# Sandwich layer on one core: 68 pages instead of 71, three more in a branch, and another order for the batches' ends

## The chip, the cores and the metric

The kernel runs on one core of a Trainium2 chip. The metric is the device time of one execution in microseconds (us), lower is better. A profile is one execution taken by the hardware profiler; times inside it are counted from its first instruction.

## The reference, cut to what matters

The input `x` has 16 batches of 512 tokens with 256 numbers each. The layer is

```
x = x + layernorm(block_sparse_attention(layernorm(x)))
x = x + layernorm(ffn(layernorm(x)))
```

and the change lies in the second line. For each token, with `xn` the input of `ffn` after its own layer norm:

```
abel   = gelu(xn @ abel_w + abel_b)
logits = xn @ moe_gate_w + moe_gate_b           # 8 experts
topw, topi = top_k(logits, 2); topw = softmax(topw)
moe    = sum over the two of topw * (gelu(xn @ ew1[e] + eb1[e]) @ ew2[e] + eb2[e])
moe    = moe @ expm(gens[0]) @ expm(gens[1]) @ expm(gens[2])
gate   = sigmoid(concat(abel, moe) @ gc_w + gc_b)
out    = residual + abel * (1 - gate) + moe * gate
```

So there are 16 x 512 x 2 = 16384 rows for the experts. How many go to which expert depends on the data.

## The kernel before, in words

**Two stages.** `attention` walks over the batches: projections, scores, weighting, and in `close(b)` the first residual, the dense `abel` part (stored in `lin_d`), the sum (stored in `x1_d`) and `route`, which gives every row a place. The rotations are folded into the experts' second weights (`second_weights`, tiles `w2` and `eb2r`) at the end of this stage.

**Pages.** A page is 256 rows of one expert. `route(b, ...)` counts the rows of each expert over all batches so far (`count`, `filled`: pages opened per expert), opens pages as they are needed, and `close` scatters the rows to their slots in `slots_d` (line 731, an indirect DMA of POOL; eight per batch). An empty slot holds a row number out of bounds, and its row is not stored later. Eight experts with ragged ends need at most 2 x 16 x 512 / 256 + 8 - 1 = 71 pages, the constant `PAGES`.

**The expert stage.** `experts` runs over all pages, full or empty, in a Python loop that is written out in full. For a page, `fetch` reads the expert's number from `whose` into registers of SP, PE and DVE (line 1038), loads `w1` (line 1046) and the 256 rows (line 1050); `flip` transposes the rows on TensorE (line 1061) and scales them on ScalarE (line 1065); `hidden` makes one half of the hidden layer (TensorE line 1078, Gelu on ScalarE line 1086); `result` makes one half of the output (TensorE `eo` line 1096, two VectorE operations lines 1103 and 1109) and scatters it to the tokens' places in `made_d` (line 1112, POOL). Within the loop the hidden layer of page n+1 is written beside the result of page n, half by half.

**The ends of the batches.** `last[b]` is the page by which every row of batch b is sure to be made: 4(b + 1) + 6. `leave(b, ...)` is a Python generator with the closing work of batch b; each `next` writes one step into the loop. Its steps: load `x1` and `abel` (lines 1126, 1128); Gelu of `abel` and its part of the gate (lines 1134, 1138); gather the batch's rows as `moe` from `made_d` (line 1144); sum them (lines 1159, 1160); Tanh for the gate (line 1164) and mixing (lines 1167 to 1181) with the statistics of the last layer norm (lines 373, 374); a power on POOL (line 1195); the shift (lines 1198, 1201) and the norm on ScalarE (line 1203); the last sum and five stores (line 1214, `place` line 156). Every batch that is leaving takes one step per page, in the page's first half:

```python
for batch in leaving:
    next(batch, None)
if n + 2 >= PAGES:
    next(leaving[-2])
```

The last batch works in two parts of two columns each. With 71 pages, batch 14's last page is 66 and batch 15's is 70.

**What sets the order.** `tc.manual_schedule` keeps PE, DVE, ScalarE and POOL in the order in which the program is written: an instruction that waits holds up all behind it on its engine. SP, which issues nearly all plain DMAs, is not in that set: a planner orders its queue, and the queue runs in that order. `scattered` and `gathered` tell the planner which accesses to `slots_d` and `made_d` depend on each other. At the very end the kernel has an `If` on `left` (lines 1300, 1301), which holds a second version of the layer and is not entered with these inputs.

Of the kernel before, what the change touches and what calls it, by code (L numbers as in the profile page):

```python
# [58 lines left out]
EARLY_TURNS = 31  # L59
KNOWN = 32  # L60
# [7 lines left out]
def kernel(ctx: ExitStack, tc: tile.TileContext, a: dict, out: bass.AP):  # L68
# [14 lines left out]
    left = keep.tile([P, 1], I32, name="left")  # L83

# [9 lines left out]
        keep.tile([1, n], I32, name=f"whose{i}") for i, n in enumerate((KNOWN, PAGES - KNOWN))  # L94
# [48 lines left out]
    def asked(slots, i):  # L143

        lo, hi = ((0, KNOWN), (KNOWN, PAGES))[i]
        first = slots_d.bitcast(I32).rearrange("(n g) c -> n g c", g=G)[lo:hi, 0, D + 2]
        gathered(slots, nc.sync.dma_start(whose[i], first.unsqueeze(0)))

    def place(b, t, store=False, part=slice(0, 4)):

        for c, p0, blk, n in RUNS:
            if not part.start <= c < part.stop:
                continue
            here = t[p0 : p0 + n * BLK, c, :]
            there = (out if store else x)[b, blk * BLK : (blk + n) * BLK, :]
            nc.sync.dma_start(*((there, here) if store else (here, there)))
# [245 lines left out]
    def attention(lowered, slots, ffn):  # L402
# [366 lines left out]
        def route(b, lg, rows):  # L769
# [134 lines left out]
            nc.vector.tensor_copy(filled, now)  # L904
            return slot_i
# [122 lines left out]
    def experts(slots, results, judged, ffn, ready):  # L1028
# [8 lines left out]
        def fetch(n):  # L1037
            e = nc.values_load(
                whose[0][0:1, n : n + 1] if n < KNOWN else whose[1][0:1, n - KNOWN : n - KNOWN + 1],
                engines=[ENG.SP, ENG.PE, ENG.DVE],  # L1040
                min_val=0,
                max_val=E - 1,
                skip_runtime_bounds_check_because="each is below E, or 0",
            )
            w1 = four.tile([P, 2 * HID + HID // P], F32, name="w1")
            nc.sync.dma_start(w1, a["w1"][bass.ds(e, 1)].rearrange("e p c -> p (e c)"))
            rows = two.tile([P, 2, ROW], F32, name="rows", bufs=7)
            gathered(
                slots,
                nc.sync.dma_start(  # L1050
                    rows, slots_d[n * G : (n + 1) * G, :].rearrange("(j p) c -> p j c", p=P)
                ),
            )
            return e, w1, rows
# [67 lines left out]
        def leave(b, until, parts):  # L1122
# [7 lines left out]
            gate = small.tile([P, 4], F32, name="gate")  # L1130
            for half in range(2):
                cs = range(2 * half, 2 * half + 2)
                own = abel[:, 2 * half : 2 * half + 2, :]
                nc.scalar.activation(own, own, AF.Gelu)
                yield
                for c in cs:
                    junk = two.tile([P, D], F32, name="junk")
                    nc.vector.tensor_tensor_reduce(
                        junk, abel[:, c, :], gcw[0], 1.0, 0.0, ALU.mult, ALU.add, gate[:, c : c + 1]
                    )  # L1140
            moe = two.tile([P, 2, 4, W], F32, name="moe")
# [11 lines left out]
            g = small.tile([P, 2, 4], F32, name="g")  # L1153
            xi = two.tile([P, 4, D], F32, name="xi")
# [3 lines left out]
            for part in parts:  # L1158
                nc.vector.tensor_tensor(y[:, part], y[:, part], moe[:, 1, part], ALU.add)
                nc.vector.tensor_tensor(gate[:, part], gate[:, part], y[:, part, D], ALU.add)  # L1160
            yield
            for part in parts:

                nc.scalar.activation(g[:, 0, part], gate[:, part], AF.Tanh, bias=gcb, scale=0.5)
            for part in parts:
                for i, sign in ((1, -0.5), (0, 0.5)):
                    nc.vector.tensor_scalar(  # L1167
                        g[:, i, part], g[:, 0, part], sign, 0.5, ALU.mult, ALU.add
                    )


                n = part.stop - part.start
                nc.vector.tensor_tensor(
                    g[:, :, part],
                    g[:, :, part],
                    power[:, b, 1, part].unsqueeze(1).to_broadcast([P, 2, n]),
                    ALU.mult,
                )
                for c in range(part.start, part.stop):
                    for i, (t, to) in enumerate(((y, x1), (abel, xi))):  # L1180
                        nc.vector.scalar_tensor_tensor(  # L1181
                            xi[:, c, :],
                            t[:, c, 0:D],
                            g[:, i, c : c + 1],
                            to[:, c, :],
                            ALU.mult,
                            ALU.add,
                        )
                    moments(small, mv, xi[:, c, :], c)
                    if c in (0, 2):  # L1190
                        yield
# [4 lines left out]
            yield  # L1196
            for part in parts:
# [4 lines left out]
                for c in range(part.start, part.stop):  # L1202
                    nc.scalar.activation(  # L1203
                        xi[:, c, :],
                        xi[:, c, :],
                        AF.Identity,
                        bias=off[:, c : c + 1],
                        scale=rs[:, c : c + 1],
                    )
                    if c == 1:  # L1210
                        yield
            yield
            for part in parts:
                nc.vector.tensor_tensor(x1[:, part], x1[:, part], xi[:, part], ALU.add)
                place(b, x1, store=True, part=part)
            yield
# [25 lines left out]
        last = [(b + 1) * 2 * S // G + E - 2 for b in range(B)]  # L1242
        early = 2
        whole, by_two = [slice(0, 4)], [slice(0, 2), slice(2, 4)]
        until = {}
        least = one.tile([P, 4], F32, name="least")
        with tc.manual_schedule(engines={ENG.PE, ENG.DVE, ENG.Activation, ENG.Pool}):
# [7 lines left out]
            leaving = []  # L1255
            for n in range(PAGES):
                if n + 3 < PAGES:
                    fetched.append(fetch(n + 3))
                if n == KNOWN // 2:
                    asked(slots, 1)  # L1260
                if n + early in last:
                    b = last.index(n + early)
                    leaving.append(leave(b, until, whole if b + 1 < B else by_two))
                if n + 2 < PAGES:
                    xns.append(flip(fetched[n + 2][2]))
# [3 lines left out]
                for half in range(2):  # L1269
                    if n + 1 < PAGES:  # L1270
                        hidden(fetched[n + 1][1], xns[n + 1], later, half)
                    result(e, rows, h, made, half)
                    if half == 0:
                        for batch in leaving:
                            next(batch, None)
                        if n + 2 >= PAGES:
                            next(leaving[-2])
# [5 lines left out]
                elif judged and n == 4:  # L1283
                    judge(least)

            next(leaving[-1])
            for batch in leaving:
                for _ in batch:
# [102 lines left out]
```

## Time and profile before

| | us |
|---|---|
| median of 3 runs | 1401.78 (1399.41 to 1402.66) |
| the profiled execution | 1397.93 |
| its span, first to last instruction | 1396.2 |
| first `flip` of the expert stage starts | 833.41 |
| last `eo` matmuls start, take | 1353.97, 5.38 |
| mean granted TensorE clock | 0.975 of full speed |

PE is TensorE's matmuls, PEld its weight loads, DVE VectorE, ACT ScalarE, POOL GpSimd, SP the engine that issues DMAs. In a table of windows each row is one stretch of time, with the busy time of PE, PEld, DVE, ACT and POOL, then the granted clock, the busy share of the DMA engines and GB/s. A timeline row gives start, duration, engine, line, operation, the tiles it writes and reads, how many instructions were merged, and in brackets how long the engine was idle before it and who released it. A row of a line's instructions gives durations in ns (least, median, most) and first and last start. A row of a DMA queue gives packets, MB and share.

### The profile page before, as it was taken

How to read it: one execution, taken by the hardware profiler on the slowest of the kernel's cores; microseconds unless marked ns; L12 is line 12 of the kernel's file. 1: busy time of each engine (PE TensorE's matmuls, PEld its weight loads, DVE VectorE, ACT ScalarE, POOL GpSimd, SP SyncE). 2: the span in 40 equal slices, each digit the busy share in tenths (PEclk: the TensorE clock that was granted, in tenths of full speed). 3: DMA queues.
4: the chain of work that ended last, by engine and by line, in shares of the span. 5: the costliest groups of instructions: out<-in, count | busy, mean ns of one | idle time of the engine just before them, and what ended most of it. 6: DMA issues, size and time to landing. Idle time of an engine off the chain costs nothing. (4 is left out here: it accounts for less than half of the span.)

```text
span 1396.2 us, 26363 instructions
## 1 busy us (share of the span) xinstructions
PE 1318.2 (94%) x9364; PEld 924.9 (66%) x9364; DVE 837.6 (60%) x2702; ACT 710.8 (51%) x1105; POOL 424.1 (30%) x433
## 2 busy tenths in 40 slices
PE   5999999999999999999998979999999999999990
PEld 2455555556555655555554668888888888888880
DVE  4366867797667668667666623224556555565565
ACT  1556556655665555666665334344444444444441
POOL 1001133323332332333424342223333333333331
PEclk9999999999999999999999989999999999999995
DMA  9971011211121121112101556455767776677732
GB/s 264 283 180 46 32 62 58 73 40 62 55 69 46 47 69 39 69 55 70 54 36 65 215 165 216 138 170 170 246 220 237 242 244 219 225 224 248 227 113 78
DMA packets 119295, 187.46 MB, mean 134 GB/s; under 512 B 12776, under 2 KB 93300, under 8 KB 119028
## 3 DMA queue, kind: packets, MB, share of 16 engines
q1 hardware_dynamic: 104516, 149.87, 34.7%
q0 software_dynamic: 12960, 33.84, 6.7%
q10 hardware_dynamic: 1680, 1.97, 0.5%
q8 instruction: 78, 1.28, 0.4%
q14 instruction: 61, 0.50, 0.1%
HBM read 107.81 MB, written 79.66 MB: 134 GB/s over the span
## 5 line engine op out<-in xcount | busy, mean ns | idle before, releaser
L616 ACT ACTIVATE prob<-score 128x1024 f32<-128x1024 f32 x384 | 372.3, 1021 | 234.0 <-PE score L606 234.0
L1096 PE MATMUL eo<-w,hid 128*128 x1136 | 269.8, 379 | 0.0
L1078 PE MATMUL hid_ps<-xn,w 128*128 128x256 f32 x1136 | 269.7, 381 | 0.0
L1112 POOL DMA_INDIRECT made_d<-made,rows x142 | 163.7, 1152 | 334.6 <-DVE made L1109 221.2
L1096 PEld LDWEIGHTS eo<-w,hid 128*128 128x128 f32 x1136 | 215.6, 190 | 31.1
L606 PE MATMUL score<-qk 32*128 32x512 f32 (+4 forms) x2560 | 231.9, 455 | 1.3 <-DVE qk L536 0.8
L1078 PEld LDWEIGHTS hid_ps<-xn,w 128*128 128x128 f32 x1136 | 211.0, 191 | 26.9 <-ACT xn L1065 0.3
L1103 DVE TENSOR_TENSOR made<-eo,eb2r_b 128x257 f32<-128x257 f32 x142 | 60.5, 426 | 251.1 <-PE eo L1096 224.4
L1086 ACT ACTIVATE hid<-hid_ps,w 128x256 f32<-128x256 f32 x284 | 118.9, 469 | 169.9 <-PE hid_ps L1078 121.2
L627 PE MATMUL att<-prob,vals 128*32 128x512 f32 (+4 forms) x2560 | 180.0, 427 | 0.0
L606 PEld LDWEIGHTS score<-qk 32*128 32x128 f32 x2560 | 119.6, 186 | 78.9 <-issue 36.1
L627 PEld LDWEIGHTS att<-prob,vals 128*32 128x32 f32 x2560 | 76.8, 110 | 135.5 <-issue 113.6
L731 POOL DMA_INDIRECT slots_d<-rows,slot_i x128 | 127.6, 997 | 71.8 <-issue 34.9
L379 POOL TENSOR_TENSOR rs<-rs,halves 128x4 f32<-128x4 f32 x32 | 32.9, 1028 | 327.6 <-DVE rs L378 321.7
L1065 ACT ACTIVATE xn<-flip,beta,gamma 128x256 f32<-128x256 f32 x142 | 72.4, 560 | 92.8 <-PE flip L1061 83.1
L544 PE MATMUL projv<-wv,ht 128*128 128x256 f32 x256 | 64.4, 393 | 4.4 <-DVE vals L551 4.1
L637 ACT COPY outs<-att 128x512 f32<-128x512 f32 x64 | 37.5, 586 | 55.7 <-PE att L627 55.7
L536 DVE SCALAR_TENSOR_TENSOR qk<-proj,owns,added_q 128x512 f32<-128x512 f32 x64 | 45.1, 746 | 34.0 <-PE proj L526 34.0
L526 PE MATMUL proj<-ht,wq 128*128 128x512 f32 x128 | 64.9, 631 | 0.0
L716 PE MATMUL abel<-wa,xn 128*128 128x264 f32 x256 | 63.6, 393 | 0.0
L688 POOL TENSOR_TENSOR power<-spread,halves 128x8 f32<-128x8 f32 x16 | 26.6, 1662 | 119.0 <-DVE spread L684 119.0
L526 PE MATMUL proj<-hk,wk 128*128 128x512 f32 x128 | 62.5, 611 | 0.1
(247 smaller groups left out, 1522.7 us busy)
## 6 DMA issues: line engine op xcount, KB each, us to landing
w<-in_w SPq DMA_DIRECT2D x71, 514.0 KB, 5.6
slots_d<-empty SPq DMA_DIRECT2D x1, 18389.0 KB, 71.2
rows<-slots_d SPq DMA_DIRECT2D x71, 259.0 KB, 3.1
moe<-made_d SPq DMA_DIRECT2D x30, 514.0 KB, 5.0
x_d<-x SPq DMA_DIRECT2D x16, 512.0 KB, 2.6
lin_d<-lin SPq DMA_DIRECT2D x16, 512.0 KB, 3.2
x<-x_d SPq DMA_DIRECT2D x16, 512.0 KB, 7.3
abel<-lin_d SPq DMA_DIRECT2D x16, 512.0 KB, 5.5
```

The source lines that it names most:

```text
L526: nc.tensor.matmul(ps, w[:, k, u * P : (u + 1) * P], src[:, k, :], start=k == 0, stop=k == 1,)
L544: nc.tensor.matmul(ps, ht[:, k, c * P : (c + 1) * P], wv[:, k, :], start=k == 0, stop=k == 1,)
L606: nc.tensor.matmul(ps[t // 2][:, t % 2, at : at + hi - lo], k[32 * t : 32 * t + 32, c * P : (c + 1) * P], q[32 * t : 32 * t + 32, lo:hi], ...
L616: nc.scalar.activation(pr, ps[i], AF.Exp, scale=HD**-0.5)
L627: nc.tensor.matmul(po[32 * t : 32 * t + 32, lo:hi], vals[b % 2][:, c, 4 * g + t, :], got[t // 2][:, t % 2, at : at + hi - lo], start=first ...
L716: nc.tensor.matmul(ps, xn[:, k, c * P : (c + 1) * P], wa[:, k, :], start=k == 0, stop=k == 1,)
L731: scatter = nc.gpsimd.indirect_dma_start(slots_d, bass.IndirectOffsetOnAxis(slot_i[:, r, c : c + 1], 0), rows[:, r, c, :], None, bounds_ch ...
L1065: nc.scalar.activation(xn[:, k, :], ps[:, k].rearrange("p j t -> p (j t)"), AF.Identity, bias=beta[:, k : k + 1], scale=gamma[:, k : k + 1],)
L1078: nc.tensor.matmul(pair[:, m % 2, :], w1[:, k * HID + m * P : k * HID + (m + 1) * P], xn[:, k, :], start=k == 0, stop=k == 1,)
L1086: nc.scalar.activation(h[:, m, :], pair[:, m % 2, :], AF.Gelu, bias=w1[:, 2 * HID + m : 2 * HID + m + 1],)
L1096: nc.tensor.matmul(ps, h[:, m, j * P : (j + 1) * P], w2[:, bass.ds(e, 1), m, :].rearrange("p e d -> p (e d)"), start=m == 0, stop=m == HID ...
L1112: scatter = nc.gpsimd.indirect_dma_start(made_d, bass.IndirectOffsetOnAxis(rows.bitcast(I32)[:, j, D : D + 1], 0), made[:, j, :], None, bo ...
```

## The change

`MOST = 68` pages are run always. The numbers of pages 68 to 70 come from a third `whose` tile, inside a branch that runs these pages on their own, ahead of the loop, if `route` of the last batch has counted more than 68 opened pages (`opened`). The loop and `last` end at page 67, so that batch 14 closes at 66 and batch 15 at 67.

`leave` starts one page earlier and does its steps at a written pace: `paces[0]` says how many steps are taken in the first half of a page, by its distance to the batch's last page, `paces[1]` the same for the second half. `abel * power + x1` is summed into `xi` before the gather; afterwards `(y - abel) * gate` is added to it, where before `y * gate + x1` and `abel * (1 - gate)` were. The last batch's two parts are written interleaved, and its last two stores go on two queues.

```diff
+MOST = 68
@@ tile_sandwich_kernel
+    opened = keep.tile([P, 1], I32, name="opened")
-        keep.tile([1, n], I32, name=f"whose{i}") for i, n in enumerate((KNOWN, PAGES - KNOWN))
+        keep.tile([1, n], I32, name=f"whose{i}")
+        for i, n in enumerate((KNOWN, MOST - KNOWN, PAGES - MOST))
@@ place
+            queue = queues[c % len(queues)]
+            queue.dma_start(*((there, here) if store else (here, there)))
@@ route, at its end
             nc.vector.tensor_copy(filled, now)
+            if b == B - 1:
+                nc.vector.tensor_reduce(used, filled, AX.X, ALU.add)
+                nc.vector.tensor_copy(opened, used)
@@ leave
+            back = power[:, b, 1]
...
+            xi = two.tile([P, 4, D], F32, name="xi")
+            for c in range(4):
+                nc.vector.scalar_tensor_tensor(
+                    xi[:, c, :], abel[:, c, :], back[:, c : c + 1], x1[:, c, :], ALU.mult, ALU.add
+                )
+            yield
+            whole, by_two = [slice(0, 4)], [slice(0, 2), slice(2, 4)]
+            parts = whole if b + 1 < B else by_two
             moe = two.tile([P, 2, 4, W], F32, name="moe")
...
+            def gates(part):
                 nc.vector.tensor_tensor(y[:, part], y[:, part], moe[:, 1, part], ALU.add)
                 nc.vector.tensor_tensor(gate[:, part], gate[:, part], y[:, part, D], ALU.add)
+                nc.scalar.activation(g[:, part], gate[:, part], AF.Tanh, bias=gcb, scale=0.5)
+
+            def other(part):
+                nc.vector.tensor_tensor(
+                    y[:, part, 0:D], y[:, part, 0:D], abel[:, part], ALU.subtract
+                )
+                nc.vector.tensor_scalar(g[:, part], g[:, part], 0.5, 0.5, ALU.mult, ALU.add)
+                nc.vector.tensor_tensor(g[:, part], g[:, part], back[:, part], ALU.mult)
+
+            def mixed(c):
+                nc.vector.scalar_tensor_tensor(
+                    xi[:, c, :], y[:, c, 0:D], g[:, c : c + 1], xi[:, c, :], ALU.mult, ALU.add
+                )
+                moments(small, mv, xi[:, c, :], c)
+
+            def scales(part):
+                (lines 1192 and 1195)
+            def shifts(part):
+                (lines 1198 and 1201)
+            def normed_mix(c):
+                (line 1203)
+            def stored_sum(part, queues=(nc.sync,)):
+                nc.vector.tensor_tensor(x1[:, part], x1[:, part], xi[:, part], ALU.add)
+                place(b, x1, store=True, part=part, queues=queues)
+
+            if b + 1 < B:
+                part = parts[0]
+                gates(part)
+                yield
+                other(part)
+                mixed(0)
+                yield
+                mixed(1)
+                mixed(2)
+                yield
+                mixed(3)
+                scales(part)
+                yield
+                shifts(part)
+                normed_mix(0)
+                normed_mix(1)
+                yield
+                normed_mix(2)
+                normed_mix(3)
+                yield
+                stored_sum(part)
+                yield
+            else:
+                first, second = parts
+                gates(first)
+                other(first)
+                mixed(0)
+                mixed(1)
+                scales(first)
+                gates(second)
+                other(second)
+                shifts(first)
+                normed_mix(0)
+                normed_mix(1)
+                mixed(2)
+                mixed(3)
+                scales(second)
+                stored_sum(first)
+                shifts(second)
+                normed_mix(2)
+                normed_mix(3)
+                stored_sum(second, (nc.sync, nc.scalar))
+                yield
@@ experts, the loop
-        last = [(b + 1) * 2 * S // G + E - 2 for b in range(B)]
-        early = 2
+        last = [min((b + 1) * 2 * S // G + E - 2, MOST - 1) for b in range(B)]
+        paces = [{k: 1 for k in range(-3, 2)}, {}]
+        paces[0].update({2: 3, 3: 2, 4: 2})
+        paces[1].update({4: 1})
+        more = nc.values_load(opened[0:1, 0:1], min_val=0, max_val=PAGES)
+        with tc.If(more > MOST), tc.manual_schedule(engines=in_order):
+            asked(slots, 2)
+            for n in range(MOST, PAGES):
+                e, w1, rows = fetch(n)
+                xn = flip(rows)
+                h = two.tile([P, HID // P, G], F32, name="hid")
+                made = four.tile([P, 2, W], F32, name="made")
+                for half in range(2):
+                    hidden(w1, xn, h, half)
+                for half in range(2):
+                    result(e, rows, h, made, half)
+            def go_on(n, half):
+                for b in leaving:
+                    for _ in range(paces[half].get(n - last[b], 0)):
+                        next(leaving[b])
+
-            for n in range(PAGES):
+            for n in range(MOST):
...
-                if n + early in last:
-                    b = last.index(n + early)
-                    leaving.append(leave(b, until, whole if b + 1 < B else by_two))
+                if n + 3 in last:
+                    b = last.index(n + 3)
+                    leaving[b] = leave(b, until)
...
                     result(e, rows, h, made, half)
-                    if half == 0:
-                        for batch in leaving:
-                            next(batch, None)
-                        if n + 2 >= PAGES:
-                            next(leaving[-2])
+                    if n + 1 < MOST:
+                        go_on(n, half)
...
-            next(leaving[-1])
-            for batch in leaving:
-                for _ in batch:
+            go_on(MOST - 1, 0)
+
+            next(leaving[B - 1])
+            for b in range(B):
+                for _ in leaving[b]:
                     pass
```

## The prediction

> **What bounds the kernel now.** I read the page first, then windows over the expert stage, then the timeline at the stage's start, in the middle of a batch and at its end, and last the line of an existing branch.
>
> ```profile
> PE 1318.2 (94%) x9364; PEld 924.9 (66%) x9364; DVE 837.6 (60%) x2702; ACT 710.8 (51%) x1105; POOL 424.1 (30%) x433
> ```
> ```profile
> 1100.00:1200.00 100.00, 100.00 (x489) 87.64 (x488) 58.06 (x169) 45.64 (x102) 35.87 (x31) 1.00 0.72 228
> 1200.00:1300.00 100.00, 100.00 (x490) 87.64 (x490) 54.58 (x160) 48.20 (x108) 36.98 (x32) 1.00 0.74 237
> ```
> TensorE is the bound of the expert stage: busy 100 of 100 us at the full granted clock, VectorE (third pair) at 55 to 58, ScalarE at 46 to 48. A page's block starts with its `flip`: flips stand at 1193.99 and 1201.36, so one page costs 7.37 us. What is worth time is a page less, or a stall of TensorE.
>
> ```profile
> 807.74 16.37 PEld L1013 LDWEIGHTS w2r<-rot,w2t 128*128 128x128 f32 x76
> 827.22 0.98 POOL L731 DMA_INDIRECT slots_d<-rows,slot_i  x1 [0.30 <-issue]
> 830.38 3.44 SPq L1050 DMA_DIRECT2D rows<-slots_d  x7
> 833.41 1.94 PE L1061 MATMUL flip<-ident,rows 128*128 128x128 f32 x8 [8.89 <-DMA rows<-slots_d]
> ```
> At the stage's start TensorE is idle from 824.1 to 833.4: it waits for the last scatter into `slots_d` to land, then for the first `rows`.
>
> ```profile
> 1353.97 5.38 PE L1096 MATMUL eo<-w,hid 128*128 x24
> 1364.80 0.43 DVE L1103 TENSOR_TENSOR made<-eo,eb2r_b 128x257 f32<-128x257 f32 x1
> 1366.27 2.09 POOL L1112 DMA_INDIRECT made_d<-made,rows  x1 [0.20 <-issue]
> 1369.62 1.91 SPq L1144 DMA_DIRECT2D moe<-made_d  x4
> 1373.18 0.70 DVE L1159 TENSOR_TENSOR moe<-moe 128x514 f32<-128x514 f32 x1 [2.04 <-DMA moe<-made_d]
> 1387.86 0.69 DVE L1214 TENSOR_TENSOR x<-x,xi 128x512 f32<-128x512 f32 x1 [0.29 <-ACT xi L1203]
> ```
> Call the last matmul's end E (1353.97 + 5.38 = 1359.35). The last `made` comes only 5.4 us later, because VectorE, in written order, does batch 14's sums first. Then scatter, gather and batch 15's arithmetic follow in one chain; the last sum ends at 1388.55, E + 29.2, and the span at E + 36.85.
>
> **Does the branch stay untaken?** The reference's routing on its inputs sends 3849, 1182, 1593, 809, 3068, 1176, 2250 and 2457 rows to the eight experts. In pages of 256, rounded up: 16 + 5 + 7 + 4 + 12 + 5 + 9 + 10 = 68, not over 68. The trace says the same. From 1350 to 1397 the queue of indirect transfers moves nothing:
> ```profile
> q0 software_dynamic: 289, 0.00, 0.4%
> ```
> At 48 packets each that is six scatters, those of pages 68 to 70: they carry no row.
>
> **Three pages less.** 3 x 7.37 = 22.1 us of TensorE that nothing else overlaps: E comes 22.1 us earlier.
>
> **The branch.** Each engine gets a register load, a compare and a jump over the three pages. The kernel has such a jump at its end:
> ```profile
> L1301 PEldq COMPARE_BRANCH  x1: 3357/3357/3357, 1357.1 to 1357.1; - x1
> L1301 ACTq COMPARE_BRANCH  x1: 50/50/50, 1387.2 to 1387.2; - x1
> ```
> The row first: 3.36 us on TensorE; on ScalarE 0.05, but its next entry on that line is at 1389.7, 2.5 us later. The Trainium skill ("Runtime: NRT & Kernel Launch", section "Instruction fetch mechanics") gives the reason and speaks against the change: a taken branch beyond the fetched pages waits for an instruction fetch, and control flow at run time is expensive. By that rule alone I would add 3.4 us. By the trace the place matters: TensorE has 9.3 idle us there, so load (0.31) and jump (3.36) after 824.1 end near 828, before 833.4. SP can read the count at about 818.5, when the last routing is done, and is through by about 822.5; its first three loads of `w` (5.6 us to land; issued near 780 before) go out near 823.5 and are there before the first rows. POOL jumps after its last scatter and needs 0.5 + 2.5 + 1.35 (`INC_SWDGE_SEM` of the same line), near 833, and is needed at 846. What is left on the path is VectorE's reduce and copy ahead of the last eight scatters: 2 x 0.2 = 0.4 us. If the cover fails (`rows` waiting for POOL's jump, or `w` late) it is 3 to 4 us. A gain is excluded: the first flip waits for a scatter that comes no earlier. I take +0.4.
>
> **The middle batches.** The arithmetic changes by one 128x1024 subtraction (1.23 us by the row of `moe<-moe`) less two small operations: about +1 us of VectorE per batch, free at 58%. The pace is not free. The gather `moe` still goes out in the page after the batch's last one, but its sum and the Tanh now stand one page earlier. Batch 9, pages 48 and 49:
> ```profile
> 1193.99 0.60 PE L1061 MATMUL flip<-ident,rows 128*128 128x128 f32 x4
> 1195.42 0.98 SPq L1144 DMA_DIRECT2D moe<-made_d  x2
> 1197.54 0.57 SPq L1126 DMA_DIRECT2D x<-x_d  x1
> 1198.09 0.43 DVE L1103 TENSOR_TENSOR made<-eo,eb2r_b 128x257 f32<-128x257 f32 x1 [0.87 <-PE eo L1096]
> 1203.52 1.90 PE L1096 MATMUL eo<-w,hid 128*128 x8
> ```
> The second gather goes out near 1195.9 and lands 5.0 us later, 1200.9. VectorE is free for the sum at 1198.9, so it now waits 2 us. Queued behind it is ScalarE's Tanh, and behind that the next batch's Gelu and the Gelu of page 49's second half, which TensorE's `eo` at 1203.52 needs at its third of four parts (1204.5). Landing 1200.9 + sums 1.5 + Tanh 0.25 + Gelu 0.5 + Gelu 0.45 = 1203.6: 0.9 us to spare. Batches differ. Where the two gathers are issued 1.7 us apart (three of the 14 batches that close among pages, at 1048, 1136 and 1254) it lands 1.3 us later, and TensorE waits 0.3 to 1.2 us, 2.7 together; the others add a few tenths. Over 14 batches I take +3.3 us. With all landings 1 us earlier it is 0.4; with all 1 us later 13. Stores and `made` have room: four `eo` buffers are two pages.
>
> **The end.** Batches 14 and 15 now close one page apart, so almost nothing of batch 14 is covered. Its gather is written after both scatters of the last page, and in the trace a gather waits for every scatter written before it (batch 9's went out at 1195.42, with the landing of page 47's first scatter, though its rows were in by page 46). Relative to E: the last `made` 1.6 (no batch-14 sums ahead, three to four us better), scatter issued 2.35, landed 3.25 later (1366.27 to 1369.5 before) = 5.6; gather issued by 6.1, landed 5.2 later = 11.3. Batch 14: sum and gate 1.45, subtraction 1.25, three small 0.4, four columns of 1.08 (0.48 + 0.43 + 0.18) = 4.3, scale, POOL's power and shift 1.9, four Identity 2.3, sum 1.25: ends at 24.2. VectorE is in written order, so batch 15 (landed long since) starts there: first half 0.9 + 0.7 + 0.4 + 2.15 + 0.2, the second half's gates and shifts 2.3, columns 2.15, power and shift 1.6, Identity 1.3, sum 0.7: about 12.3, ends at 36.4 against 29.2. The last two stores now go on two queues right behind it (0.6 against 1.84 from last sum to last issue): -1.2. Net +5.9. If the gather of 14 starts before the last scatter it is 3; if gathers disturb each other 9.
>
> **Sum.** -22.1 + 0.4 + 3.3 + 5.9 = -12.5 us. The profiled execution took 1397.93 (span 1396.2 and 1.7 around it), which becomes 1385.4. It is 3.85 below the median of the runs, so I put the difference on the median: 1401.78 - 12.5 = 1389.3.
>
> **The rivals.** *Nearly the whole gain*: gathers land a little earlier, no stalls, and the end costs only 2 to 3: -22.1 + 0.4 + 2.5 = -19, 1382.6. For it: batch 15 alone is 3 us shorter by its new order. Against it: batch 14 has lost its cover of four pages.
>
> *Slower, by the gather.* The next batch's loads of `x1` and `abel` (1 MB) are now written in the same step as the gather; before, `x` came out behind it (1197.54). If they go out just ahead, 1 MB at the 230 GB/s of this window is 4.4 us of transfers, of which 2 us would fall on the gather. Each batch then stalls TensorE about 2 us more at the Tanh: 3.3 + 14 x 1.8 = 28, the sum is +12, 1414. It decides from 1.2 us of lateness per batch. Against it: SP waits at the gather for the scatter anyway, and transfers issued before that wait are mostly done by its end.
>
> *The branch is taken.* Expert 4 holds 3068 rows of 3072; five rows routed otherwise would open a 69th page. Three pages without overlap, at 10 to 15 us each, cost 30 to 45: 1425. The empty scatters above speak against it.
>
> *Less*: jump exposed or later landings, -3 to -7, near 1397.
>
> **How the numbers follow.** About 0.2% (2.8 us) is what a measurement of this kernel can tell from none. My forecast (-17 to -7): 0.55. Nearly the whole gain: 0.18. Less, but faster: 0.08. Within 0.2%: 0.04. Slower by the gather: 0.13; branch taken: 0.02. So faster 0.81, same 0.04, slower 0.15. The range leaves out the slower cases and the best twentieth: 1380 to 1399; the likeliest case's own is 1385 to 1395.
>
> **What would show it.** 68 of each page group, 1088 `eo` matmuls; TensorE from the first flip to E 22 us shorter less its stalls; those stalls, if any, at `eo` released by ScalarE in the third page after a batch's last; first flip within 1 us of 833.4; the Tanh's idle time put down to the gate sum and that one's to `moe<-made_d`; batch 14's gather issued near E + 6 and the last sum near E + 36. Wrong would be a first flip past 836, stalls over 10 us together, or a last sum before E + 31.

## The result, and the profile after

The changed kernel took 1407.86 us (median of 12 runs, 1402.62 to 1410.11); the kernel before, on the same chip, 1402.70 (12 runs, 1399.41 to 1405.35). The ratio is 1.0027, 95% interval 1.0014 to 1.0040: slower by 0.27% or some 4 us (the medians lie 5.2 us apart), where 12.5 us less were forecast. The profiled execution took 1402.62, with a span of 1400.8 against 1396.2.

The page's first row, and the two windows in the middle of the stage (columns as in the tables of windows before):

```profile
PE 1297.2 (93%) x9256; PEld 904.4 (65%) x9256; DVE 844.9 (60%) x2692; ACT 700.7 (50%) x1088; POOL 409.8 (29%) x427
```
```profile
1100.00:1200.00 100.00, 100.00 (x491) 87.46 (x490) 60.69 (x168) 46.41 (x106) 32.85 (x30) 1.00 0.74 239
1200.00:1300.00 100.00, 99.72 (x487) 87.07 (x486) 60.45 (x173) 47.00 (x106) 34.91 (x31) 1.00 0.72 227
```

TensorE's busy time fell by 21.0 us: the three pages are gone. The middle is still nearly full; 0.28 us of idle time shows in the second window. So most of the time went at the two ends of the stage. The start of the stage (timeline):

```profile
832.74 0.98 POOL L735 DMA_INDIRECT slots_d<-rows,slot_i  x1 [0.30 <-issue]
835.71 0.34 SPq L1135 DMA_DIRECT2D x<-x_d  x1
...
837.52 0.74 SPq L1135 DMA_DIRECT2D x<-x_d  x1
844.12 0.36 SPq L1055 DMA_DIRECT2D w<-in_w  x1
844.53 0.43 SPq L1059 DMA_DIRECT2D rows<-slots_d  x1
...
848.57 1.09 PE L1070 MATMUL flip<-ident,rows 128*128 128x128 f32 x4 [18.86 <-DMA rows<-slots_d]
```

and, of the instructions of the branch's line, these five rows (duration in ns, first and last start in us; an `EVENT_SEMAPHORE` is a wait of an engine's queue, a `COMPARE_BRANCH` the jump):

```profile
L1300 SPq EVENT_SEMAPHORE  x8: 17/17/17, 838.8 to 843.5; - x8
L1300 PEldq COMPARE_BRANCH  x1: 358/358/358, 827.3 to 827.3; - x1
L1300 ACTq COMPARE_BRANCH  x1: 50/50/50, 830.6 to 830.6; - x1
L1300 POOLq INC_SWDGE_SEM  x1: 618/618/618, 833.0 to 833.0; - x1
L1300 SPq COMPARE_BRANCH  x1: 50/50/50, 838.3 to 838.3; - x1
```

Before, SP sent out the first `rows` 3.16 us behind the start of the last scatter, as soon as it had landed. After, it is 11.79 us (832.74 to 844.53), and these parts add up to it. SP stands 2.97 us in its queue until the scatter has landed, because loads of `x1` and `abel` for batches 0 to 2 are now ahead of the jump, and they too wait for the scatters; 2.60 us go to issuing five of them (835.71 to 838.31); 5.19 us to the waits behind SP's jump (838.31 to 843.5), which end one by one (at 839.4, 840.6, 841.9 and 843.3); 1.03 us to the expert's number and the first `w`. That these waits are for the five loads is read from their number and order; this trace does not show the loads' landings. The trace of e3, with the same branch, does for some: there two of the waits are passed at 835.59 and 836.90, and two of the loads land at 835.58 and 836.89. TensorE, ScalarE and POOL jumped long before, as the prediction had it. SP did not.

The way from the first `flip` to the first `eo` grew as well, by 2.8 us. Of these 2.0 are a second wait of TensorE, ahead of the second page's `flip` (851.66). The rest are slower matmuls: the first 16 of `hid_ps` take 5.80 us, where they took 5.07. They run longer at a low granted clock, the third number from a row's end in these stretches, two of the kernel before (first `flip` at 833.41) and two of the changed one (848.57). The clock is back at full some 4.6 us behind the first `flip` before, and 8.4 after.

```profile
834.00:838.00 4.00, 4.00 (x14) 3.13 (x13) 0.00 (x0) 3.21 (x5) 0.00 (x0) 0.50 1.01 319
838.00:842.00 4.00, 4.00 (x22) 3.54 (x21) 0.00 (x0) 2.45 (x6) 0.00 (x0) 0.99 1.02 410
```
```profile
850.00:854.00 4.00, 2.33 (x8) 2.10 (x9) 0.00 (x0) 3.24 (x6) 0.00 (x0) 0.50 1.00 366
854.00:858.00 4.00, 4.00 (x14) 3.24 (x13) 0.00 (x0) 2.01 (x3) 0.00 (x0) 0.63 1.05 385
```

The end of the stage, some rows from the last matmuls on:

```profile
1352.74 5.54 PE L1105 MATMUL eo<-w,hid 128*128 x24
1358.32 0.43 DVE L1112 TENSOR_TENSOR made<-eo,eb2r_b 128x257 f32<-128x257 f32 x1 [0.22 <-PE eo L1105]
1359.65 1.01 POOL L1121 DMA_INDIRECT made_d<-made,rows  x1 [0.30 <-issue]
1364.71 3.12 SPq L1163 DMA_DIRECT2D moe<-made_d  x6
1369.94 1.23 DVE L1178 TENSOR_TENSOR moe<-moe 128x1028 f32<-128x1028 f32 x1 [8.54 <-DMA moe<-made_d]
1393.53 0.69 DVE L1219 TENSOR_TENSOR x<-x,xi 128x512 f32<-128x512 f32 x1 [1.22 <-ACT xi L1210]
```

Batch 14's sums wait for their gather (8.54 us of idle VectorE), and batch 15's work stands behind them. The last sum ends at E + 35.9, where it was E + 29.2.

A second profile of the changed kernel was taken later (e7, below). The whole by stages, where "scatter" is the start of the last scatter into `slots_d`, E the end of the last matmul and "sum" the end of the last sum (us; differences of the rows of each timeline):

| | before | after | again |
|---|---|---|---|
| start to last scatter | 827.2 | 832.7 | 828.6 |
| scatter to first `flip` | 6.2 | 15.8 | 16.2 |
| first `flip` to first `eo` | 8.9 | 11.8 | 10.9 |
| first `eo` to E | 517.0 | 497.9 | 503.7 |
| E to last sum | 29.2 | 35.9 | 36.4 |
| last sum to end | 7.6 | 6.6 | 6.8 |

The first row's 5.5 us do not belong to the change: the second profile has 1.4, and e1's, with the same first stage, 0.1. In the profiles of the experiments below the last scatter starts between 823.7 (e12) and 834.9 (e9); what sets it was not tried. The second profile is from another chip, where the kernel before took 1394.31 us (median of 15 runs), so its 1404.38 us lie 10 us above that kernel.

### The profile page after: what moved, and what is told of

Same layout as the page of the kernel before. It is cut to its first block, busy times and chain, and to the rows that moved or that the text cites. A ratio compares the mean times of both kernels' runs of the same rounds, so it can differ in the third digit from the quotient of the medians.

```text
span 1400.8 us, 26082 instructions
## 1 busy us (share of the span) xinstructions
PE 1297.2 (93%) x9256; PEld 904.4 (65%) x9256; DVE 844.9 (60%) x2692; ACT 700.7 (50%) x1088; POOL 409.8 (29%) x427
## 3 DMA queue, kind: packets, MB, share of 16 engines
q8 instruction: 78, 1.28, 0.4%
## 5 line engine op out<-in xcount | busy, mean ns | idle before, releaser
L1105 PE MATMUL eo<-w,hid 128*128 x1088 | 259.5, 380 | 1.9 <-ACT hid L1095 1.9
L1087 PE MATMUL hid_ps<-xn,w 128*128 128x256 f32 x1088 | 259.1, 381 | 0.0
L1121 POOL DMA_INDIRECT made_d<-made,rows x136 | 146.7, 1079 | 324.0 <-DVE made L1118 264.5
L1105 PEld LDWEIGHTS eo<-w,hid 128*128 128x128 f32 x1088 | 206.1, 190 | 33.2 <-ACT hid L1095 3.7
L1087 PEld LDWEIGHTS hid_ps<-xn,w 128*128 128x128 f32 x1088 | 202.8, 191 | 25.7
L1095 ACT ACTIVATE hid<-hid_ps,w 128x256 f32<-128x256 f32 x272 | 113.6, 469 | 112.4 <-PE hid_ps L1087 72.1
L1074 ACT ACTIVATE xn<-flip,beta,gamma 128x256 f32<-128x256 f32 x136 | 69.3, 561 | 54.1 <-PE flip L1070 47.1
```

What stands on the lines that cost most here:

```text
L1074: nc.scalar.activation(xn[:, k, :], ps[:, k].rearrange("p j t -> p (j t)"), AF.Identity, bias=beta[:, k : k + 1], scale=gamma[:, k : k + 1],)
L1087: nc.tensor.matmul(pair[:, m % 2, :], w1[:, k * HID + m * P : k * HID + (m + 1) * P], xn[:, k, :], start=k == 0, stop=k == 1,)
L1095: nc.scalar.activation(h[:, m, :], pair[:, m % 2, :], AF.Gelu, bias=w1[:, 2 * HID + m : 2 * HID + m + 1],)
L1105: nc.tensor.matmul(ps, h[:, m, j * P : (j + 1) * P], w2[:, bass.ds(e, 1), m, :].rearrange("p e d -> p (e d)"), start=m == 0, stop=m == HID ...
L1121: scatter = nc.gpsimd.indirect_dma_start(made_d, bass.IndirectOffsetOnAxis(rows.bitcast(I32)[:, j, D : D + 1], 0), made[:, j, :], None, bo ...
```

## The experiments

**Theory A**: the branch costs about 10 us through SP's queue, in which other loads were put ahead of the jump and the branch waits for their landing. **Rival B**: the branch is cheap, and the gathers' stalls and the longer end eat the gain. **Rival C**: the code that stands between (skipped instructions, tables loaded anew) costs the time, whatever SP does.

**e1: no branch.** The changed kernel without the branch, so without pages 68 to 70.

```diff
-        more = nc.values_load(opened[0:1, 0:1], min_val=0, max_val=PAGES)
-        with tc.If(more > MOST), tc.manual_schedule(engines=in_order):
-            ...
```

> The changed kernel with the branch left out (its condition is false with these inputs, so the same pages run). Theory A (the join is the loss: SP's loads of x1 and abel stand ahead of its jump, and w and rows come only after them): first flip back to about 6 us after the last scatter's issue (15.8 in the changed kernel), first eo 12 us earlier, all else as in the changed kernel: about 1407.9 - 12.5 = 1395, or 1390 if the 5 us by which the first stage ran late in the changed kernel go with it. Theory B (the new pace and the longer end are the loss): time stays near 1405, first flip moves but the gain is lost later.

1391.19 us (11 runs) against 1397.85 (16 runs) of the kernel before on the chip of e1 to e4; ratio 0.9950 (0.9927 to 0.9973). Scatter to first `flip` is 5.8, to first `eo` another 9.1: the start is as before. E to last sum is 36.3. The waits of TensorE have

```profile
PE eo L1105 <- ACT hid L1095: 7.2, 7, 3.0
```

(us in total, times, longest), and first `eo` to E is 504.5, 9.6 more than 517.0 - 22.1. So without the branch the change gains half a per cent: the ratio goes from 1.0027 to 0.9950, about 11 us (each ratio against the kernel before on its own chip; the changed kernel was not timed on this one). The end and the stalls of B are real, but they leave a gain.

**e2: the loads held.** The branch stays; the loads of `x1`, `abel` and of the second `whose` may not be queued ahead of the third page's `rows`.

```diff
+            if n == 2:
+                behind_pages.append(got.ins.name)
...
-            nc.sync.dma_start(x1, x1_d[b])
+            after_pages(nc.sync.dma_start(x1, x1_d[b]))
...
-            nc.sync.dma_start(abel, lin_d[b])
+            after_pages(nc.sync.dma_start(abel, lin_d[b]))
```

> The changed kernel with the branch, but the x1 and abel loads and the load of the later pages' numbers are ordered in SP's queue behind the third page's rows. Theory A: SP jumps near 825 instead of 838, w goes out near 829 and the rows with the last scatter's landing, first flip 6 to 7 us after the last scatter's issue; the two extra table loads on ScalarE and the cold clock stay (about 2.5 us): 1407.9 - 9 = 1399. Theory A2 (any jump costs this much, by instruction fetch or by the waits of its skipped arm, whatever stands before it): no gain, 1407.

1391.08 us (6 runs), ratio 0.9936 (0.9915 to 0.9958): the same as with no branch, and less than the 1399 that theory A gave. Four rows of the branch, to be read against those of the changed kernel above:

```profile
L1312 SPq EVENT_SEMAPHORE  x8: 17/17/17, 820.7 to 821.3; - x8
L1312 PEldq COMPARE_BRANCH  x1: 358/358/358, 822.7 to 822.7; - x1
L1312 ACTq COMPARE_BRANCH  x1: 50/50/50, 826.1 to 826.1; - x1
L1312 SPq COMPARE_BRANCH  x1: 50/50/50, 820.2 to 820.2; - x1
```

The same eight waits take 0.6 us in place of 4.7, since none of SP's loads is in flight ahead of them, and SP's jump stands 7.9 us ahead of the last scatter's start (828.1), where it stood 5.6 us behind it. Scatter to first `flip` is 6.0. That decides for A over C: code and jumps are unchanged, only the queue's order is not. What stays is the way to the first `eo`, 11.2 in place of 8.9 (e9 to e12), and TensorE's waits in the middle:

```profile
PE eo L1117 <- ACT hid L1107: 6.0, 6, 3.8
```

**e3: the branch alone.** The kernel before, all 71 pages, with such a branch (entered over 70 opened pages) and nothing else.

```diff
+        more = nc.values_load(opened[0:1, 0:1], min_val=0, max_val=PAGES)
+        with tc.If(more > PAGES - 1), tc.manual_schedule(engines={...}):
+            (pages 68 to 70)
```

> The kernel before with the branch alone (71 pages in the loop as before, the old leave; the branch holds the pages 68 to 70 once more and is not entered). Theory A: the loads are put ahead of the jump here too: +10 to +13, about 1414. Theory B: +0 to +2.

1408.06 us (6 runs), ratio 1.0063 (1.0039 to 1.0087), some 9 us more (10.2 between the medians). Its scatter to first `flip` is 16.7 and its first `flip` to first `eo` 11.4, while the stage from there to E is 517.05, as before to within 0.1. So the price belongs to the branch and to the start of the stage. Three rows of its branch:

```profile
L1256 SPq EVENT_SEMAPHORE  x8: 17/17/17, 832.5 to 837.2; - x8
L1256 PEldq COMPARE_BRANCH  x1: 358/358/358, 820.2 to 820.2; - x1
L1256 SPq COMPARE_BRANCH  x1: 50/50/50, 832.3 to 832.3; - x1
```

**e4: the gather earlier.** On e2: the gather is written at the end of the batch's last page in place of the first half of the page behind it, and the steps after it stay.

```diff
-        paces = [{k: 1 for k in range(-3, 2)}, {}]
+        paces = [{k: 1 for k in range(-3, 1)}, {}]
...
-        paces[1].update({4: 1})
+        paces[1].update({0: 1, 4: 1})
```

> As e2_loads_held, and the gather of a batch is written at the end of its last page instead of after the next page's first scatter. If the gather's wait for that later scatter is what makes the Tanh late: gather issued about 4 us after the next page's start instead of 8.8, no idle of TensorE at eo by ScalarE (3 us gained with its waits), and batch 14's gather issued about 3 us earlier at the end: 5 to 6 us below e2_loads_held, about 1393. If the lateness comes from the DMA engines' load, the landing moves by less and the gain is under 2.

1383.57 us (6 runs), ratio 0.9891 (0.9868 to 0.9913), 7.5 us below e2's median on the same chip. First `eo` to E is 496.1 where e2 has 502.9, and the wait of `eo` is nearly gone:

```profile
PE eo L1117 <- ACT hid L1107: 0.8, 1, 0.8
```

That is the stall of the middle batches, found and removed: the Tanh starts 7.4 us into its page in the mean over the batches, where it was 9.4 in e2, and hardly holds up the Gelu behind it any more. The end gains too: E to last sum is 34.3 in place of 36.2.

**e5: the table early.** On e4, a Gelu of one column written first in the last region, so that its table would be there before the first page.

```diff
+            hot = one.tile([P, 1], F32, name="hot")
+            nc.scalar.activation(hot, ident[:, 0:1], AF.Gelu)
             fetched = [fetch(n) for n in range(3)]
```

> As e4_gather_earlier, with one Gelu of a 128x1 constant written as ScalarE's first operation behind the branch. In the kernels with a branch the first eo comes 11.2 us after the first flip, without it 9.0, and ScalarE loads a table twice, the first one standing ahead of the first xn. If that is the 2.2 us: the table is loaded while TensorE still waits for rows, no second load, first eo 9 us after the first flip, about 2 us below e4_gather_earlier. If the slow first flips (cold clock) are the cause: no change.

1390.21 us (10 runs), ratio 0.9962 (0.9947 to 0.9978): a miss, 0.7% worse than e4. The Gelu was put ahead of the branch, among the copies of `w2`, and it waits for the scatters into `slots_d`; that its tile takes memory which they still read is the likely reason, not shown:

```profile
817.78 0.37 ACT L1029 COPY w<-w2r 128x257 f32<-128x257 f32 x1 [0.49 <-PE w2r L1022]
831.12 1.28 ACT L1325 ACT_TABLE_LOAD   x1 [12.97 <-DMA slots_d<-rows,slot_i]
```

ScalarE stood for 13 us, the copies behind it too, and TensorE waited 11.7 us for them. It says nothing on the table.

**e6: the ends woven.** On e5, the closing steps of batches 14 and 15 are taken alternately (5, 2, 2, 1, 1 of them, then the rest), as far as the order of the two gathers allows.

```diff
-            for b in range(B):
-                for _ in leaving[b]:
-                    pass
+            for batch, steps in (
+                (one_before, 5), (very_last, 2), (one_before, 2), (very_last, 1), (one_before, 1),
+            ):
+                for _ in range(steps):
+                    next(batch)
+            (then the rest of both)
```

> As e5_table_early, and the ends of batches 14 and 15 are written woven: the first gates of batch 15 while batch 14 waits for POOL's power, its columns while batch 14 waits for ScalarE's norm. If VectorE's written order is what makes the end long (36 us from the last matmul to the last sum in the changed kernel): 3 to 4 us off the 34.3 of e4_gather_earlier. If the end is bound by the gathers' landing: under 1 us.

1388.87 us (6 runs), ratio 0.9944 (0.9925 to 0.9963). E to last sum is 31.4 against 34.5 of e5: batch 15's first half fills the time in which batch 14 waits for POOL's power and ScalarE's norm. In the runs' times 1.3 us of it show, within their spread.

**e7: the changed kernel again**, one run with a profile.

> The changed kernel once more, for its profile alone: its first stage ended 5.5 us later than in the kernel before. If that belongs to the program, the last scatter into slots_d is issued near 832.7 again; if it belongs to that one execution, near 827. The first flip comes 15.8 us after it in both cases, by theory A.

1404.38 us; its stages are in the table above. The start of the stage repeats (16.2 and 10.9), the first 828 us do not, and the stalls are larger: `eo` waits longer for ScalarE. First the first profile, then this one:

```profile
PE eo L1105 <- ACT hid L1095: 1.9, 3, 1.0
PE eo L1105 <- ACT hid L1095: 5.4, 5, 2.2
```

The clock has a share in it. Right behind the longest of these waits (2.2 us, up to 984.3) the granted clock is at half from 985.1 to 988.5, and the eight matmuls of `hid_ps` at 985.34 take 3.49 us in place of 1.89. No such drop shows in the middle of the first profile, nor in e1 and e2, which have waits of 3.0 and 3.8 us.

**e9: woven without the early Gelu**, on e4.

> The kernel with the held loads and the earlier gather, and the ends of the last two batches woven as before, without the early Gelu. My theory: the parts add up, since each acts at a place of its own. First flip 5.9 us behind the last scatter, first eo 11.2 behind the first flip (the two table loads are still behind the join), E less first eo 496 to 497, the last sum E + 31.4 where it was E + 34.3: some 3 us below the kernel with the earlier gather, ratio to the kernel before about 0.987. Rival: the weaving only gained because the early Gelu had moved other things; then sum - E stays at 34 and the ratio at 0.989.

**e10: the table kept**, on e9: the small Gelu reads the last copied piece of `w2` and writes a tile of its own.

```diff
+            nc.scalar.activation(hot, w2[:, E - 1, HID // P - 1, 0:1], AF.Gelu)
             fetched = [fetch(n) for n in range(3)]
```

> The same, with one Gelu of a single column that reads the last copied piece of w2, so that it cannot run before the last copy, and writes a tile of its own. My theory: it stands behind ScalarE's jump and its table load falls into the time in which ScalarE waits for the first rows (from about 831 to 834), so that no table load is left between the first flip and the first eo: eo less flip 9.0 as before in place of 11.2, all else as in the kernel beside it, 2 us less, ratio about 0.9855. Rival: the load of the table was not on the path to the first eo, and the 2 us are the slower first flip (1.1 us in place of 0.6); then eo less flip stays at 11 and the ratio equals that of the kernel beside it.

e9: 1387.43 us (6 runs), ratio 0.9887 (0.9861 to 0.9913), E to last sum 30.7. e10: 1387.87 (6 runs), ratio 0.9894 (0.9867 to 0.9921), 30.6. The weaving holds without the Gelu, in the profile; e9's ratio is e4's all the same, so 3 us at the end are not resolved by these runs. In the profiles the first stage hides them: the last scatter starts at 834.9 in e9 and 834.4 in e10, where e4, on another chip, has 827.3. In e10 the table load is out of the way, yet first `flip` to first `eo` is 11.7, as in e9 (11.9): the rival was right that the load alone did not set it. The rows of e10 show what did:

```profile
835.09 1.28 ACT L1327 ACT_TABLE_LOAD   x1 [0.71 <-issue]
...
837.58 0.38 SPq L1070 DMA_DIRECT2D rows<-slots_d  x1
838.59 0.36 SPq L1068 DMA_DIRECT2D w<-in_w  x1
839.00 0.42 SPq L1070 DMA_DIRECT2D rows<-slots_d  x1
840.01 0.35 SPq L1068 DMA_DIRECT2D w<-in_w  x1
...
840.52 1.08 PE L1083 MATMUL flip<-ident,rows 128*128 128x128 f32 x4 [8.88 <-DMA rows<-slots_d]
...
843.82 1.09 PE L1083 MATMUL flip<-ident,rows 128*128 128x128 f32 x4 [2.21 <-DMA rows<-slots_d]
```

TensorE's second `flip` waits 2.21 us for the second page's rows. Behind the branch SP asks in written order: `w`, `rows`, `w`, `rows`; the first `rows` waits for the scatters, so the next two `w` go out between the rows. Before, nothing but rows went out then. That the `w` delay the second page's rows is what e11 and e12 try.

**e11 and e12: the weights first.** On e10 and on e9: SP asks for three pages' `w` right behind its jump, then for the rows.

```diff
-            fetched = [fetch(n) for n in range(3)]
+            ahead = [weights_of(n) for n in range(3)]
+            fetched = [fetch(n, ahead[n]) for n in range(3)]
```

> As the kernel with the table kept, but SP asks for the weights of the first three pages right behind its jump, and then for the first seven pages' rows; before, each page's weights stood behind the page before's rows and so behind the last scatter. My theory now: the two to three us between first flip and first eo are the second page's flip, which waits 2.2 us for its rows, since two pages' weights share the transfers with them. With the weights out near 822 to 824 the second flip follows the first at once (0.3 us or less), and with no table load on the way either first eo less first flip is 9.0 to 9.2 in place of 11.7. Ratio to the kernel before about 0.987. Rival: what costs is TensorE's low clock after its pause, whatever the rows do; then eo less flip stays near 11.

> As the woven kernel without the early Gelu, with the same order of SP's loads. It shows whether the table load ahead of the first xn costs anything once the rows are early: if both were on the path, the first matmul of hid_ps now waits for xn, and first eo less first flip is about 10.3 (9.0 and one load of 1.28); if the load is hidden behind the second page's flip, it is 9.0 to 9.3. Ratio to the kernel before 0.987 to 0.988.

e11: 1377.18 us (6 runs) against 1394.69 (11 runs) of the kernel before on that chip, ratio 0.9870 (0.9843 to 0.9897). e12: 1377.80 (6 runs), ratio 0.9878 (0.9853 to 0.9903). First `flip` to first `eo` is 9.3 in e11, and 11.8 in e12, which is more than either reading of its expectation allowed. Two rows of e11's start, then e12's:

```profile
833.68 1.94 PE L1093 MATMUL flip<-ident,rows 128*128 128x128 f32 x8 [10.77 <-DMA rows<-slots_d]
835.55 5.43 PE L1110 MATMUL hid_ps<-xn,w 128*128 128x256 f32 x16
```

```profile
829.14 3.48 SPq L1079 DMA_DIRECT2D rows<-slots_d  x7
832.13 1.94 PE L1092 MATMUL flip<-ident,rows 128*128 128x128 f32 x8 [11.11 <-DMA rows<-slots_d]
833.36 1.28 ACT L1096 ACT_TABLE_LOAD   x1 [11.93 <-DMA rows<-slots_d]
835.27 6.66 PE L1109 MATMUL hid_ps<-xn,w 128*128 128x256 f32 x16 [1.21 <-ACT xn L1096]
```

Both pages' flips now run as one group of 8 in 1.94 us, as before the change. In e12 the hidden layer then waits 1.21 us for `xn`, which waits for the table load, and it runs longer (6.66 against 5.43 in e11): the granted clock comes back to full 9.1 us behind the first `flip`, in e11 5.4. So there are two costs side by side, the second page's rows and the table load: removing one alone (e10, e12) shows nothing, removing both (e11) shows 2.4 us. Half of e12's price is thus the clock and not the wait itself. Without e5 and e6, where ScalarE held TensorE up, the clock is at full 4.6 to 5.4 us behind the first `flip` where TensorE does not pause again (before, e1, e11), and 7.0 to 9.1 where it pauses for 1.2 to 2.3 us ahead of the hidden layer (the changed kernel twice, e2 to e4, e9, e10, e12); most of that difference is the pause. So the rival of a low clock holds in part: for half of e12's price, and for little of e10's, whose flips and first 16 matmuls of `hid_ps` take 7.66 us against 7.37 in e11. That the wait for `xn` brought on e12's long low clock was not tried on its own. e11's start has a price as well: the first rows go out 4.94 us behind the start of the last scatter (5.44 in e12), not 3.15 as in e10; three loads of weights are in flight beside the last scatters, the likely cause. So the net gain at the start is 0.6 us (scatter to first `eo`: 17.2 against 17.8), and e9 to e12 cannot be told apart in their ratios. All four are 1.1% to 1.3% below the kernel before, e11 with the lowest ratio.

## Why the prediction was wrong, and where it was right

**The failed step is the branch: +0.4 forecast, some 9 to 12.5 us measured.** The step said that SP "can read the count at about 818.5 ... and is through by about 822.5" and that its three loads of `w` would then go out. It reads the count about when forecast, right behind the last routing (824.0, with this execution's first stage 5.5 us later). But its jump came 14 us after that read. The prediction took SP's queue of the old timeline and put a jump into it; SP's queue is ordered by the planner, and the loads of `x1` and `abel`, which stood behind the rows before (833.86 on), were independent of the branch and went ahead of it. The jump inherited their wait for the scatters, and the skipped arm then waited for their landing. Scatter to first `flip` grew by 9.7 and 10.1 us in the two profiles, first `flip` to first `eo` by 2.8 and 2.0. e1 (the branch out, 0.77% better), e3 (the branch alone, 0.63% worse) and e2 (the same branch, only the queue's order changed, as good as none) show it from three sides. The bound given for a failed cover, 3 to 4 us, was drawn from two other failures and was too small as well. The prediction's own sign of being wrong, a first `flip` past 836, came (848.57).

A warning stood in the kernel before. The prediction read two rows of the branch at that kernel's end, TensorE's and ScalarE's; these two of SP stand beside them:

```profile
L1301 SPq EVENT_SEMAPHORE  x9: 17/17/17, 1393.1 to 1393.7; - x9
L1301 SPq COMPARE_BRANCH  x1: 53/53/53, 1390.4 to 1390.4; - x1
```

There too SP's waits behind its jump end 3.3 us after it. For SP's waits behind the jump the prediction's sum had no term.

**The rule on jumps.** The trace-based reading was right to give the jump itself little: TensorE's took 0.36 us here against 3.36 at the kernel's end, and no engine's jump but SP's was on the path. The Trainium skill ("Runtime: NRT & Kernel Launch", section "Instruction fetch mechanics") gave a reason to expect a wait at the jump where its target lies beyond the code already fetched. The 3.4 us that the prediction weighed by it do not show over three pages; whether their end lay within the fetched code, no run here shows. The waits behind SP's jump are another matter: they shrink from 4.7 to 0.6 us when only the loads ahead of the jump are moved (e2).

**The stalls of the middle batches were under-sized: 3.3 forecast, 3.0 to 9.6 measured.** First `eo` to E shows, against 517.0 - 22.1 = 494.9, 3.0 us in the first profile, 8.8 in the second, and 9.6 and 8.0 in e1 and e2, which share this code. The first profile was a lucky one. The mechanism is the one named, a late gather that holds the Tanh and with it the Gelu: e4, which only moves the gather, takes the time down to 1.2. The term's own sensitivity had it (13 us with all landings 1 us later); the step from one examined batch to all was too kind. The rows named for `hid` hold 1.9 of the 3.0 us and 5.4 of the 8.8; of the rest of the 8.8, 1.6 are the eight matmuls at half clock, and what is left lies in no row.

**Right**: the reduce and copy ahead of the last eight scatters (0.4 forecast; from batch 14's last scatter to batch 15's it is 13.1 us in place of 12.8); three pages are worth 22.1 us (e4 reaches 20.9 of it with 0.8 us of stall left); the branch is not entered; the end, +7.2 forecast from E to the last sum and measured +6.7 and +7.2, with the gather of batch 14 issued at E + 6.4 (forecast 6.1); the last stores, -1.2 forecast and about -1.0 and -0.9 measured; the rival by which each batch's loads of `x1` push back its gather did not come true in that size.

With the measured terms (pages, first `flip`, first `eo`, stalls, end) the sum is -22.1 + 9.7 + 2.8 + 3.0 + 5.8 = -0.8 us by the first profile, and -22.1 + 10.1 + 2.0 + 8.8 + 6.4 = +5.2 by the second. With the first stage's 5.5 and 1.4 us this is 4.7 and 6.6, where the spans differ by 4.6 and 6.4. The ratio's 0.27% is 3.8.

What stays open: why the stalls differ by 6 us from one execution of the same code to the next. In the means over the batches the Tanh starts 8.95 us into its page in the first profile, 9.24 in the second, 9.4 and 9.5 in e2 and e1 (7.4 in e4). The stalls stand in the same order but for the second profile's 8.8 us against e2's 8.0, and without the 1.6 us of half clock it would be 7.2. What moves the Tanh was not tried.

## What to carry to other kernels

When a branch is put into a queue that a planner orders, ask what the planner can move ahead of it: anything independent goes there, and the jump then inherits its waits, while the arm that is skipped may still wait for the landing of what is in flight. Read the queue's order in the changed program, not in the old timeline, and look at every engine's rows of a branch that is already there. And when removing one cause changes nothing, look for a second that was hidden behind it before calling the first innocent.

## What the runs showed of the hardware that was not expected

- A skipped arm costs more than its jump. SP's compare took 0.05 us in all runs; its eight waits took 4.7 to 5.7 us where five or six loads were queued ahead of it (changed kernel twice, e3) and 0.5 to 1.1 us where none were (e2, e4 to e6, e9 to e12).
- The jump of TensorE over three pages took 0.36 us in every profile with the branch, against 3.36 us for the one at the kernel's end.
- Behind the branch ScalarE loads its tables twice (1.28 us each, one ahead of `xn` and one ahead of the Gelu), where the kernel before and e1 load one there; one early Gelu behind the branch leaves a single load (e10).
- With three weight loads in flight the way from the last scatter's start to the first rows was 4.9 and 5.4 us (e11, e12), without them 3.2 (before, e10).
- A short pause can cost more than itself: behind one wait of 2.2 us the granted clock was at half for 3.4 us, and eight matmuls took 3.49 us in place of 1.89 (e7). Longer waits in e1 and e2 drew no such drop.
